# A two-layer graph network on one core: edge coefficients kept between two passes, shorter leftovers, and one edge tile in 75 fetched row by row from SyncE's queue

## The chip, the cores and the metric

The kernel runs on one core of a Trainium2 chip. The metric is device time in microseconds (us) of one execution. The engines are TensorE (PE; its weight loads are written PEld), VectorE (DVE), ScalarE (ACT), GpSimd (POOL) and SyncE (SP). "SPq" and "ACTq" in the profile are the instruction queues of SP and ACT, from which plain DMAs are issued; DMAs with an index list are issued by POOL.

## The reference

There are 30,000 nodes with 128 features and 960,000 edges, sorted by destination. Layer 0 has two relation passes, layer 1 one gate pass; each has a sum over edges by destination.

```
def _rel_graph_conv(h, basis, coeff, bias, src, dst, etype, norm):
    W = einsum('rb,bdf->rdf', coeff, basis)        # 32 relations of 8 bases
    msg = einsum('nd,rdf->nrf', h, W)[src, etype] * norm
    return segment_sum(msg, dst) + bias

h = max(layernorm(x), 0)
x = x + rel(relu(rel(h, basis1, coeff1, bias1)), basis2, coeff2, bias2)
h = max(layernorm(x), 0)
for t in range(4):
    eta = sigmoid((h @ Wk[t] + bk[t])[dst] + (h @ Wq[t] + bq[t])[src])
    agg = segment_sum(where(type4 == t, eta * (h @ Wv[t] + bv[t])[src], 0), dst)
    outs.append(agg + h @ Ws[t] + b[t])
x = x + mean(outs)
```

Both relation passes use the same sources, destinations, 32 edge types and edge weights; only the table of node rows, the bases and the 32 x 8 coefficients differ.

## The kernel before

**Tiles and groups.** An edge tile is 128 edges, a group is G = 3 tiles, a block is S = 5 groups, a stage is 5 blocks (25 groups, 75 tiles), and a turn of the loop is 4 stages (100 groups). A pass is a loop of 25 turns (L312). There are three passes, each made by `edge_pass` (L296): "c1" and "c2" with `rel_body` (L367), and "g" with `gate_body`. Turns go from the highest destinations to the lowest. The sums stay in SBUF, in the tile `agg`, with features on partitions and nodes along the free dimension.

**A group of a relation pass** (L438 to L467). POOL gathers three tiles of 128 rows into `hg` (L442, through the helper at L114); there are five `hg` buffers. DVE builds for each tile `sb`, a one-hot of the destination within a 32-node window times the 8 basis coefficients of each edge (L446). PE multiplies `hg` with `sb` into `pa` (L452), ACT copies `pa` into `ab` (L456). Once a block, PE multiplies the 8 bases into `po` (L414), and DVE adds the five windows into `agg` (L365).

**The coefficients of a block** (L383 to L409). SP loads the edge types, repeated over 32 partitions, into `er` (two buffers, L385); DVE compares them with the partition's number (L392); PE multiplies this one-hot with the coefficient table into `cp` (L397); DVE multiplies with the edge weights into `ce` (L406). The load is issued two blocks ahead. Both passes do this.

**Beside the edges.** Each turn also finishes ten blocks of 120 nodes whose sums are complete, one step at a time between the groups (`beside`, L323): after c1, ReLU and the row store to `h1`; after c2, layer norm and the matmuls that make the tables `ktab` and `qvtab`, which ACT's queue stores (L660); after g, the store of the output (L698). What is left after the last turn, 1440 nodes or 12 blocks, is done behind the loop, block by block (L328 to L332), before the next pass begins.

**What orders the work.** Each engine runs its instructions in the order in which this code names them. At the start of a stage SP loads the indices (`idx`), window positions (`relc`), weights (`nrm`) and window bases (`firsts`) of the next stage; the first stage's are loaded at the start of the turn (L419). At the third block of a stage each engine waits until all engines have left the stage before (L433). Waits are set by the recording layer. Each DMA that SP or ACT issues is given one of eight completion counters (called DMAHW0 to DMAHW7 in the built program) in turn, over both queues, and waits until the last DMA of that counter is complete; the counters are a set for each stage.

Of the kernel before, what the change touches and what calls it, by code (L numbers as in the profile page):

```python
# [9 lines left out]
F32 = mybir.dt.float32  # L10
I32 = mybir.dt.int32
# [7 lines left out]
P = 128  # L19
D = 128  # L20
# [27 lines left out]
LAG = 2 * VB  # L48
NX = N + NPI + LAG
GAP = 8  # L50
EPS = 1e-5
CH = 5
IN_RANGE = "destinations are node numbers, below N"
# [16 lines left out]
def kernel(  # L70
# [40 lines left out]
    qidx = nc.dram_tensor("qidx", (TP, NT), I32, kind="Internal").ap()  # L111

# [30 lines left out]
    basis, coeff = [], []  # L143
    for i, (bas, cof) in enumerate(((basis1, coeff1), (basis2, coeff2))):
        ct = consts.tile([P, 4, B], F32, name=f"coeff{i}")
        nc.vector.memset(ct, 0.0)
        for q in range(4):
            nc.scalar.dma_start(ct[q * R:(q + 1) * R, q, :], cof)
        basis.append(bas)
        coeff.append(ct)  # L150
# [34 lines left out]
    with tc.tile_pool(name="prep", bufs=2) as prep, tc.tile_pool(name="pre", bufs=4) as pre, \  # L185
# [52 lines left out]
        last = prep.tile([NI, 1], F32, name="last", bufs=1)  # L238
        nc.vector.tensor_reduce(last, at, AX.X, ALU.max)
        even = prep.tile([NI, 1], F32, name="even", bufs=1)  # L240
        nc.gpsimd.iota(even, pattern=[[0, 1]], base=N + LAG - W, channel_multiplier=-NPI,
                       allow_small_or_imprecise_dtypes=True)
        late = prep.tile([NI, 1], F32, name="late", bufs=1)
        nc.vector.tensor_tensor(late, last, even, ALU.is_gt)
# [4 lines left out]
    n_bad = nc.values_load(flag[0:1, 0:1], min_val=0, max_val=2 * CH * TP + NI)  # L249
# [44 lines left out]
    def sorted_path():  # L294
        with ExitStack() as all_:
            def edge_pass(name, body, after, banks, extra=None):  # L296


                with ExitStack() as held:
                    weights = held.enter_context(tc.tile_pool(name=f"{name}_w", bufs=1))  # L300
                    steps, run = after(weights), body(weights)
                    with tc.tile_pool(name=f"{name}_io", bufs=NQ) as io, \
                            tc.tile_pool(name=f"{name}", bufs=2) as pool, \
                            tc.tile_pool(name=f"{name}_n", bufs=1) as npool, \
                            tc.tile_pool(name=f"{name}_nps", bufs=banks, space=PSUM) as nps, \
                            tc.tile_pool(name=f"{name}_c", bufs=1, space=PSUM) as cps, \
                            tc.tile_pool(name=f"{name}_ps", bufs=2, space=PSUM) as ps:
                        cp = cps.tile([P, 4 * D], F32, name="cp")
                        iw, ic = cp[:, :W], cp[:, W:W + 1]
                        nc.vector.tensor_copy(iw, irow)  # L310
                        nc.vector.tensor_copy(ic, icol)
                        with tc.For_i(0, NI, 1, iteration_sync="staggered") as i:  # L312
                            with tc.manual_schedule():
                                todo = {}
                                for n, step_ in extra(i, npool) if extra else ():
                                    todo.setdefault(n, []).append(step_)
                                for u in range(NPI // VB):
                                    at = i * -NPI + (N + LAG + u * VB)
                                    for n, step in steps(at, npool, nps):
                                        todo.setdefault(u * PERIOD + n, []).append(step)  # L320
                                assert W < TQ * 4 * B and max(todo) < NG
# [6 lines left out]
                    with tc.tile_pool(name=f"{name}_l", bufs=3) as lpool, \  # L328
                            tc.tile_pool(name=f"{name}_lps", bufs=6, space=PSUM) as lps:
# [26 lines left out]

            def edge_row(row, i, s, n):
# [9 lines left out]
            def rel_body(table, weights, cof):  # L367
# [5 lines left out]
                def body(bas, i, io, pool, ps, cp, iw, ic, beside):  # L373
                    stage = {}
                    er, oh, pc, ce, ab, po, base = {}, {}, {}, {}, {}, {}, {}

                    def loads(k):
                        stage[k] = [stage_tile(io, "idx", src, I32, i, k),
                                    stage_tile(io, "relc", reld, F32, i, k),
                                    stage_tile(io, "nrm", norm, F32, i, k, 4 * TQ - S * G),  # L380
                                    firsts(io, i, k)]

# [7 lines left out]
                    def onehot(s):  # L390
                        oh[s] = pool.tile([P, TQ, TP], F32, name="oh")
                        nc.vector.tensor_scalar(oh[s], er[s], icol4, None, op0=ALU.is_equal)  # L392
                        at = (1 + s % 2) * TQ * 4 * B
                        pc[s] = cp[:TP, at:at + TQ * 4 * B].rearrange("p (c q b) -> p c q b",
                                                                      c=TQ, q=4)
                        for c in range(TQ):
                            nc.tensor.matmul(pc[s][:, c].rearrange("p q b -> p (q b)"),  # L397
                                             lhsT=oh[s][:, c, :],
                                             rhs=cof.rearrange("p q b -> p (q b)"),
                                             start=True, stop=True)  # L400

                    def coefficients(s):
                        ce[s] = pool.tile([TP, 4, TQ, B], F32, name="ce")
                        t0 = s % SB * S * G
                        nrm = stage[s // SB][2][:, t0:t0 + 4 * TQ]
                        nc.vector.tensor_mul(  # L406
                            ce[s], pc[s].rearrange("p c q b -> p q c b"),
                            nrm.rearrange("p (q c) -> p q c", q=4).unsqueeze(3).to_broadcast(
                                [TP, 4, TQ, B]))  # L409
# [10 lines left out]
                    types(0)  # L420
                    onehot(0)
                    coefficients(0)
                    types(1)
                    onehot(1)
                    for s in range(NS):
# [8 lines left out]
                        idx, relc, _, start = stage[k]  # L434
                        if s + 2 < NS:
                            types(s + 2)
                        ab[s] = pool.tile([P, B, S, W], F32, name="ab")
                        for g in range(S):  # L438
                            t0 = (s % SB * S + g) * G
                            hg = pool.tile([TP, G, D], F32, name="hg", bufs=5)  # L440
                            for j in range(G):
                                gather(hg[:, j, :], table, idx[:, t0 + j:t0 + j + 1])  # L442
                            pa = ps.tile([P, B, W], F32, name="pa", bufs=3)
                            for j in range(G):
# [4 lines left out]
                                    ce[s].rearrange("p q c b -> p (q c) b")[  # L449
                                        :, g * G + j, :].unsqueeze(2).to_broadcast([TP, B, W]),  # L450
                                    op0=ALU.is_equal, op1=ALU.mult)
                                nc.tensor.matmul(pa.rearrange("p b w -> p (b w)"),  # L452
                                                 lhsT=hg[:, j, :],
# [5 lines left out]
                            if g == 2 and s + 1 < NS:  # L459
                                coefficients(s + 1)  # L460
                            if g == 3 and s + 2 < NS:
                                onehot(s + 2)
# [100 lines left out]
            def after_first(weights):  # L563

                def steps(at, pool, ps):
                    xt = pool.tile([VB, D], F32, name="xt", bufs=2)
# [27 lines left out]
            def after_second(weights):  # L594
# [9 lines left out]
                def steps(at, pool, ps):  # L604
                    cols, rows = agg[:, ds(at, VB)], ds(at, VB)
                    xs = pool.tile([P, VB], F32, name="xs", bufs=2)
# [73 lines left out]
            def after_third(weights):  # L680

                def steps(at, pool, ps):
# [51 lines left out]
            edge_pass("c1", rel_body(h0, basis[0], coeff[0]), after_first, 2, codes)  # L734
            edge_pass("c2", rel_body(h1, basis[1], coeff[1]), after_second, 2)
# [3 lines left out]
    def any_path():  # L739
        with ExitStack() as all_:  # L740
# [60 lines left out]
            def rel_conv(table, to, weights, cof, relu):  # L801
                bas = cs.tile([P, B, D], F32, name="bas", bufs=2)
                nc.scalar.dma_start(bas, weights.rearrange("b d f -> d b f"))
                with tc.tile_pool(name="slow", bufs=2) as pool, \
# [18 lines left out]
                    for j in range(G):  # L823
                        nc.tensor.matmul(pc[:, j, :], lhsT=oh[:, j, :], rhs=cof[:R, 0], start=True,
                                         stop=True)
# [24 lines left out]
            rel_conv(h0, agg1, basis[0], coeff[0], False)  # L850
            rel_conv(agg1, agg2, basis[1], coeff[1], True)
# [117 lines left out]
```

## Time and profile before

| what | value |
|---|---|
| median of 3 runs | 28697.99 us (28687.42 to 28701.98) |
| the profiled execution: time | 28695.83 us |
| the profiled execution: span | 28694.1 us |
| first gather of c1, of c2, of g | 193.03, 9671.56, 19211.24 us |
| last gather of c1, of c2, of g ends | 9627.03, 19087.42, 28665.14 us |
| mean granted TensorE clock | 0.725 |
| DMA queues: of POOL's gathers; of SP; of ACT | 26.3%, 10.8%, 3.1% of 16 engines |

The span is the time from the first to the last instruction in the profile; the execution's time has 1.7 us more. In a group's line of the profile, "busy, mean ns" is the time in which the engine worked on it, and "idle before" is the time in which the engine stood just before it, with what ended most of that. "issue" means that the profile shows nothing that the engine waited for. A timeline line has the start in us, the duration, the engine and the line, and in brackets the idle time before it.

### The profile page before, as it was taken

The numbers are of one execution on the slowest core, as the hardware profiler recorded it, in microseconds if no ns is written. First come the engines' busy times: TensorE is split into PE (matmuls) and PEld (weight loads), VectorE is DVE, ScalarE is ACT, GpSimd is POOL, SyncE is SP. The second block draws the span as 40 slices with busy tenths as digits, with TensorE's granted clock in tenths as the row PEclk, the third lists the DMA queues.
The fourth block names the chain that finished last, engine by engine and source line by source line (L and its number), as shares of the span: only waits on it lengthen the run. The fifth ranks groups of instructions, "written<-read, shape, count | busy, mean of one in ns | idle before, by whom it ended". The sixth has DMA issues, their size and how long they took to land. (4 is left out here: it accounts for less than half of the span.)

```text
span 28694.1 us, 321544 instructions
## 1 busy us (share of the span) xinstructions
PE 21423.9 (75%) x87408; PEld 17175.0 (60%) x87408; DVE 12662.0 (44%) x33274; ACT 3718.3 (13%) x9905; POOL 21329.2 (74%) x22514
## 2 busy tenths in 40 slices
PE   5777777777777777777777777777777777777777
PEld 3555555555555555555555555556666666666666
DVE  4444444444444444444444444444444444444444
ACT  2111111111111111111111111111111111111111
POOL 5777777777777777777777777767777777777777
PEclk8888888888888888888888888875555555555555
DMA  4222222222222333333333333335555555555555
GB/s 113 73 74 73 73 75 74 74 74 74 74 73 74 80 88 88 88 88 88 88 87 88 87 87 88 87 107 177 176 177 177 177 176 176 177 177 177 177 177 168
DMA packets 2183600, 3244.39 MB, mean 113 GB/s; under 512 B 552518, under 2 KB 1560194, under 8 KB 2181890
## 3 DMA queue, kind: packets, MB, share of 16 engines
q0 software_dynamic: 840000, 1967.52, 26.3%
q1 hardware_dynamic: 994220, 1001.69, 10.8%
q10 hardware_dynamic: 347670, 254.20, 3.1%
q8 instruction: 852, 13.96, 0.2%
q14 instruction: 858, 7.03, 0.1%
HBM read 2969.33 MB, written 252.28 MB: 112 GB/s over the span
## 5 line engine op out<-in xcount | busy, mean ns | idle before, releaser
L114 POOL DMA_INDIRECT hg<-h,idx x15000 | 14212.2, 947 | 4846.7 <-issue 3865.1
L452 PE MATMUL pa<-sb,hg 128*128 128x256 f32 x30000 | 9879.9, 460 | 4210.1 <-DMA hg<-h,idx 2911.0
L452 PEld LDWEIGHTS pa<-sb,hg 128*128 128x128 f32 x30000 | 6016.4, 223 | 7340.5 <-issue 3683.7
L114 POOL DMA_INDIRECT qv<-qvtab,qi x7500 | 7089.3, 945 | 2488.5 <-issue 2063.6
L446 DVE SCALAR_TENSOR_TENSOR sb<-cp,relc,ce 128x256 f32<-128x256 f32 x15000 | 6145.4, 476 | 5311.9 <-PE cp L397 4980.1
L517 PE MATMUL po<-sel,msg 128*128 128x32 f32 x15000 | 3551.9, 393 | 2400.1 <-DVE msg L515 2394.2
L517 PEld LDWEIGHTS po<-sel,msg 128*128 128x128 f32 x15000 | 3396.6, 326 | 2839.2 <-DVE msg L515 2794.1
L506 PE MATMUL pk<-kw,kb 128*128 128x128 f32 x15000 | 3976.0, 438 | 137.1 <-DVE kb L493 137.1
L456 ACT COPY ab<-pa 128x256 f32<-128x256 f32 x5000 | 1860.4, 372 | 16420.0 <-PE pa L452 16227.4
L547 DVE TENSOR_TENSOR pk<-pk,qv 128x384 f32<-128x384 f32 x2500 | 1414.5, 566 | 5017.8 <-DMA qv<-qvtab,qi 3929.8
L506 PEld LDWEIGHTS pk<-kw,kb 128*128 128x128 f32 x15000 | 3468.2, 331 | 139.9 <-issue 139.9
L414 PEld LDWEIGHTS po<-ab,bas 128*128 128x128 f32 x16000 | 2859.8, 230 | 144.7 <-ACT ab L456 50.8
L414 PE MATMUL po<-ab,bas 128*128 128x160 f32 x16000 | 2883.9, 344 | 23.1 <-ACT ab L456 23.1
L365 DVE TENSOR_TENSOR agg<-agg,po 128x32 f32 x7500 | 1403.2, 187 | 1972.8 <-PE po L414 861.4
L548 ACT ACTIVATE pk<-pk 128x384 f32<-128x384 f32 x2500 | 1187.3, 476 | 7774.6 <-DVE pk L547 7739.7
L397 PEld LDWEIGHTS cp<-coeff,oh 128*128 128x128 f32 x8000 | 1313.8, 235 | 452.5 <-issue 328.0
L397 PE MATMUL cp<-coeff,oh 128*128 128x32 f32 x8000 | 1229.3, 304 | 358.8 <-DVE oh L392 358.8
L515 DVE TENSOR_TENSOR msg<-pk,qv 128x384 f32<-128x384 f32 x2500 | 1368.1, 548 | 0.0
L493 DVE TENSOR_TENSOR kb<-kb,cp 128x1920 f32<-128x1920 f32 x500 | 1072.6, 2145 | 46.7 <-issue 29.5
L644 PE MATMUL bank<-wall,hT 128*120 128x512 f32 x1572 | 911.2, 697 | 9.0 <-issue 4.6
L655 DVE TENSOR_TENSOR kt<-bank,ball 120x512 f32<-120x512 f32 x262 | 181.1, 691 | 924.7 <-PE bank L644 924.7
L392 DVE TENSOR_SCALAR oh<-er,icol 128x512 f32<-128x512 int32 x1000 | 490.6, 491 | 88.8 <-issue 62.7
(77 smaller groups left out, 3548.1 us busy)
## 6 DMA issues: line engine op xcount, KB each, us to landing
kb<-kcode SPq DMA_DIRECT2D x500, 960.0 KB
er<-in_et_row SPq DMA_DIRECT2D x1000, 256.0 KB
hg<-h,idx POOLq DMA_INDIRECT x15000
kw<-ktab SPq DMA_DIRECT2D x2500, 64.0 KB
qvtab<-qvt ACTq DMA_DIRECT2D x262, 480.0 KB, 4.3
qv<-qvtab,qi POOLq DMA_INDIRECT x7500
ktab<-kt ACTq DMA_DIRECT2D x262, 240.0 KB, 3.3
xt<-in_x SPq DMA_DIRECT2D x262, 60.0 KB, 5.0
```

The lines of the kernel that those rows point to most:

```text
L114: nc.gpsimd.indirect_dma_start(out=to, out_offset=None, in_=table, in_offset=bass.IndirectOffsetOnAxis(ap=idx, axis=0))
L365: nc.vector.tensor_add(to, to, po[:, g, :])
L397: nc.tensor.matmul(pc[s][:, c].rearrange("p q b -> p (q b)"), lhsT=oh[s][:, c, :], rhs=cof.rearrange("p q b -> p (q b)"), start=True, stop ...
L414: nc.tensor.matmul(po[s].rearrange("p s w -> p (s w)"), lhsT=bas[:, b, :], rhs=ab[s][:, b].rearrange("p s w -> p (s w)"), start=(b == 0), ...
L446: nc.vector.scalar_tensor_tensor(sb, iw[:TP].unsqueeze(1).to_broadcast([TP, B, W]), relc[:, t0 + j:t0 + j + 1], ce[s].rearrange("p q c b - ...
L452: nc.tensor.matmul(pa.rearrange("p b w -> p (b w)"), lhsT=hg[:, j, :], rhs=sb.rearrange("p b w -> p (b w)"), start=(j == 0), stop=(j == G ...
L456: nc.scalar.copy(ab[s][:, :, g, :], pa)
L506: nc.tensor.matmul(pk[n][:, j, :], lhsT=kb[n // S][:, n % S, j * TP:(j + 1) * TP], rhs=kw[n], start=True, stop=True)
L515: nc.vector.tensor_mul(msg, pk[n], qv[n][:, :, 1, :])
L517: nc.tensor.matmul(po[s][:, g, :], lhsT=msg[:, j, :], rhs=sel[s][:, g * G + j, :], start=(j == 0), stop=(j == G - 1))
L547: nc.vector.tensor_add(pk[n], pk[n], qv[n][:, :, 0, :])
L548: nc.scalar.activation(pk[n], pk[n], AF.Sigmoid)
```

## The change

1. **Coefficients of both passes in c1.** The coefficient table gets both layers' columns, so the matmul of L397 is 64 columns wide instead of 32. DVE multiplies twice, into `ce0` for c1 and `ce1`, which ACT's queue stores to a new DRAM tensor `ce2` once a block. c2 loads its coefficients from there (`kept`, on SP's queue, four buffers) and has no types, one-hots or coefficient matmuls.
2. **Edges reversed group by group** and not turn by turn, with node blocks following closer behind. 480 nodes (4 blocks) are left after each loop instead of 1440 (12 blocks), and their steps are interleaved over the four blocks, with up to 8 PSUM buffers. The check on first destinations, which chooses between the sorted path and a general one, is made for every group.
3. **One tile in 75 by rows.** The last tile of each stage in c1 and c2 isn't gathered by POOL. SP loads its 128 indices into one partition, loads them 16 at a time into registers, and issues 128 DMAs of one row (512 bytes) each, in eight parts of 16 at groups 1, 3, 6, 8, 11, 13, 16 and 18 of the stage. The tile goes to `hx` (two buffers), which the last matmul of the stage's last group reads.

The core of the diff:

```diff
-LAG = 2 * VB
-NX = N + NPI + LAG
+LAG = 4 * VB
+NX = N + LAG
+XR = 16
...
+            def row_loader(io, pool, table, array, i, k):
+                ix = io.tile([1, TP], I32, name="ix")
+                nc.sync.dma_start(
+                    ix, array[:, ds(i * (NQ * NTS) + (k + 1) * NTS - 1, 1)].rearrange("p o -> o p"))
+                got = pool.tile([TP, D], F32, name="hx")
+
+                def fetch(c):
+                    _, vals = nc.values_load_multi_w_load_instructions(
+                        ix[:, c * XR:(c + 1) * XR], engines=[SP], min_val=0,
+                        max_val=table.shape[0] - 1,
+                        skip_runtime_bounds_check_because=IN_RANGE)
+                    for p, v in enumerate(vals):
+                        nc.sync.dma_start(got[c * XR + p:c * XR + p + 1, :], table[ds(v, 1), :])
...
+                    def one_by_one(k, n):
+                        if n == 0:
+                            rest[k] = row_loader(io, pool, table, src, i, k)
+                        for c in range(TP // XR):
+                            if n == (c * (NGS - 5)) // (TP // XR) + 1:
+                                rest[k][1](c)
...
+                        for to, l in ((ce, 0), (ce_next, 1)):
+                            to[s] = pool.tile([TP, 4, TQ, B], F32, name=f"ce{l}")
+                            nc.vector.tensor_mul(
+                                to[s], pc[s][:, :, :, l].rearrange("p c q b -> p q c b"),
...
+                    def keep(s):
+                        nc.scalar.dma_start(block_rows(s), ce_next[s][:, :S * G, :].rearrange(
+                            "p t b -> p (t b)"))
+
+                    def kept(s):
+                        ce[s] = pool.tile([TP, S * G, B], F32, name="ce", bufs=4)
+                        nc.sync.dma_start(ce[s].rearrange("p t b -> p (t b)"), block_rows(s))
...
                             hg = pool.tile([TP, G, D], F32, name="hg", bufs=5)
+                            rows = [hg[:, j, :] for j in range(G)]
+                            if t0 + G == NTS:
+                                rows[-1] = rest[k][0]
                             for j in range(G):
-                                gather(hg[:, j, :], table, idx[:, t0 + j:t0 + j + 1])
+                                if t0 + j + 1 < NTS:
+                                    gather(rows[j], table, idx[:, t0 + j:t0 + j + 1])
...
-                        for at in range(0, NPI + LAG, VB):
-                            for _, step in steps(at, lpool, lps):
+                        for together in zip(*(steps(at, lpool, lps, left)
+                                              for at in range(0, LAG, VB))):
+                            for _, step in together:
                                 step()
```

More of the change, by code (lines that the diff above doesn't have):

```diff
@@ L47 @@
 PERIOD = NG * VB // NPI - 1
-LAG = 2 * VB
-NX = N + NPI + LAG
+LAG = 4 * VB
+NX = N + LAG
+LEAD = 3 * VB
 GAP = 8
 EPS = 1e-5
+XR = 16
 CH = 5
-IN_RANGE = "destinations are node numbers, below N"
+IN_RANGE = "the edges' ends are node numbers, below N"
 def rows_of(col, n):
@@ L111 @@
     qidx = nc.dram_tensor("qidx", (TP, NT), I32, kind="Internal").ap()
+    ce2 = nc.dram_tensor("ce2", (NI * NS, TP, S * G * B), F32, kind="Internal").ap()
     def gather(to, table, idx):
@@ L141 @@
     nc.vector.memset(eps, EPS)
[L143 to L146, printed above, removed]
+    basis = basis1, basis2
+    coeff = consts.tile([P, 4, 2, B], F32, name="coeff")
+    nc.vector.memset(coeff, 0.0)
+    for i, cof in enumerate((coeff1, coeff2)):
         for q in range(4):
-            nc.scalar.dma_start(ct[q * R:(q + 1) * R, q, :], cof)
-        basis.append(bas)
-        coeff.append(ct)
+            nc.scalar.dma_start(coeff[q * R:(q + 1) * R, q, i, :], cof)
     def normalised(pool, xt, kn, name, p=P):
@@ L237 @@
         nc.sync.dma_start(at, first.rearrange("(i g) -> i g", i=NI))
[L238 to L242, printed above, removed]
+        even = prep.tile([NI, NG], F32, name="even", bufs=1)
+        nc.gpsimd.iota(even, pattern=[[-NPI // NG, NG]], base=N + LAG - LEAD - W,
+                       channel_multiplier=-NPI, allow_small_or_imprecise_dtypes=True)
+        nc.vector.tensor_tensor(even, at, even, ALU.is_gt)
         late = prep.tile([NI, 1], F32, name="late", bufs=1)
-        nc.vector.tensor_tensor(late, last, even, ALU.is_gt)
+        nc.vector.tensor_reduce(late, even, AX.X, ALU.add)
         nc.vector.tensor_add(nbad[:NI], nbad[:NI], late)
@@ L294, in sorted_path @@
     def sorted_path():
+        for u in range(NPI // VB):
+            late = min(g for g in range(NG)
+                       if min((g // S + 2) * S + S - 2, NG) > u * PERIOD + 1)
+            assert (u + 1) * VB - late * NPI // NG <= LEAD
         with ExitStack() as all_:
@@ L317, in edge_pass @@
                                 for u in range(NPI // VB):
-                                    at = i * -NPI + (N + LAG + u * VB)
-                                    for n, step in steps(at, npool, nps):
+                                    at = i * -NPI + (N + LAG - (u + 1) * VB)
+                                    for n, step in steps(at, npool, nps, 2):
                                         todo.setdefault(u * PERIOD + n, []).append(step)
-                                assert W < TQ * 4 * B and max(todo) < NG
+                                assert W < TQ * 8 * B and max(todo) < NG
                                 def beside(n):
@@ L365, in add_windows, with rel_body @@
                     nc.vector.tensor_add(to, to, po[:, g, :])
-            def rel_body(table, weights, cof):
+            def rel_body(table, weights, second):
                 def start(npool):
@@ L374, in body @@
                     stage = {}
-                    er, oh, pc, ce, ab, po, base = {}, {}, {}, {}, {}, {}, {}
+                    er, oh, pc, ce, ce_next, ab, po, base, rest = {}, {}, {}, {}, {}, {}, {}, {}, {}
                     def loads(k):
@@ L379, in loads @@
                                     stage_tile(io, "relc", reld, F32, i, k),
-                                    stage_tile(io, "nrm", norm, F32, i, k, 4 * TQ - S * G),
                                     firsts(io, i, k)]
+                        if not second:
+                            stage[k].append(
+                                stage_tile(io, "nrm", norm, F32, i, k, 4 * TQ - S * G))
+                    def one_by_one(k, n):
[4 more added lines that the diff above has]
+                                rest[k][1](c)
                     def types(s):
@@ L402, in coefficients @@
                     def coefficients(s):
-                        ce[s] = pool.tile([TP, 4, TQ, B], F32, name="ce")
                         t0 = s % SB * S * G
[L405 to L409, printed above, removed]
+                        nrm = stage[s // SB][-1][:, t0:t0 + 4 * TQ]
@@ L419, in body @@
                     loads(0)
[L420 to L424, printed above, removed]
+                    if second:
+                        kept(0)
+                        kept(1)
+                    else:
+                        types(0)
+                        onehot(0)
+                        coefficients(0)
+                        types(1)
+                        onehot(1)
                     for s in range(NS):
@@ L433, in body @@
                             leave_stage()
-                        idx, relc, _, start = stage[k]
+                        idx, relc, start = stage[k][:3]
                         if s + 2 < NS:
-                            types(s + 2)
+                            (kept if second else types)(s + 2)
                         ab[s] = pool.tile([P, B, S, W], F32, name="ab")
@@ L458, in body @@
                                 bases_out(s - 1)
-                            if g == 2 and s + 1 < NS:
+                            if g == 2 and not second and s + 1 < NS:
                                 coefficients(s + 1)
-                            if g == 3 and s + 2 < NS:
-                                onehot(s + 2)
+                            if g == 3 and not second:
+                                keep(s)
+                                if s + 2 < NS:
+                                    onehot(s + 2)
                             if g == 3 and s > 1:
@@ L680, in after_third, with steps @@
             def after_third(weights):
-                def steps(at, pool, ps):
+                def steps(at, pool, ps, deep):
                     c = pool.tile([P, VB], F32, name="c")
@@ L823, in rel_conv @@
                     for j in range(G):
-                        nc.tensor.matmul(pc[:, j, :], lhsT=oh[:, j, :], rhs=cof[:R, 0], start=True,
+                        nc.tensor.matmul(pc[:, j, :], lhsT=oh[:, j, :], rhs=cof, start=True,
                                          stop=True)
@@ L917, in edges @@
     def edges(v):
-        return np.ascontiguousarray(v.reshape(NI, -1)[::-1]).reshape(-1)
+        return np.ascontiguousarray(v.reshape(NGR, GE)[::-1]).reshape(-1)
     def by_tile(v):
```

45 lines of the change are left out of this document (26 added, 19 removed).

## The prediction, made before the changed kernel ran

> **What bounds the kernel.** First the page's busy table and its costliest groups. No engine is near full, yet GpSimd (POOL) has a row of its own kind:
>
> ```profile
> PE 21423.9 (75%) x87408; PEld 17175.0 (60%) x87408; DVE 12662.0 (44%) x33274; ACT 3718.3 (13%) x9905; POOL 21329.2 (74%) x22514
> ...
> L114 POOL DMA_INDIRECT hg<-h,idx x15000 | 14212.2, 947 | 4846.7 <-issue 3865.1
> ...
> L114 POOL DMA_INDIRECT qv<-qvtab,qi x7500 | 7089.3, 945 | 2488.5 <-issue 2063.6
> ```
>
> 22,500 gathers of 947 ns busy and about 0.30 us between them. POOL's timeline in mid pass shows that the 0.30 is no wait but the pace itself:
>
> ```profile
> 5000.97 0.94 POOL L114 DMA_INDIRECT hg<-h,idx  x1 [0.30 <-issue]
> 5002.22 0.94 POOL L114 DMA_INDIRECT hg<-h,idx  x1 [0.31 <-issue]
> 5003.47 0.95 POOL L114 DMA_INDIRECT hg<-h,idx  x1 [0.30 <-issue]
> ```
>
> First to last gather, the first relation pass (c1) takes 9434.0 us (193.03 to 9627.03), the second (c2) 9415.9 (9671.56 to 19087.42), the gate pass 9453.9: 1.256 us a gather, 3.77 a group of three. These three stretches and the gaps of 44.5 and 123.8 us between them are the span. So POOL's gathers bound all three passes, and what counts is any time that POOL must wait.
>
> **What goes.** (a) One gather in 75 in c1 and c2: 200 x 1.256 = **-251 us**, all of it on the path. (b) The node blocks left after each loop go from 12 to 4 and are interleaved. In the gap before the gate pass 12 blocks run one behind the other from 19097.8 to 19198.4, 100.6 us. Four together keep the first block's 3.4 us up to its first L644, four times about 4.8 us of PE work (six L644 rows of 697 ns and the small ones) and an end of some 5 us: about 28, so -72. The gap before c2 has 16.8 us of blocks (9636.1 to 9652.9), the end 14.4 (28675.8 to 28690.2); a third of each plus one chain leaves 6 and 5: -11 and -9. Together **-92 us**.
>
> **What is hidden.** c1 gets a second multiplication per block (L406 takes 0.28 us), wider coefficient matmuls (L397, 304 ns each) and a store; c2 loses L392, L397, L406 and 500 loads of 256 KB. All are on engines that idle in every block (DVE 44% busy), so nothing either way; if c1's DVE cover were gone, 500 x 0.28 = 140 us. As traffic, 25,600 rows of 512 B and c2's 500 coefficient loads come, 128 MB of type loads go; POOL's waits for landed gathers are 265 us in 702 times, 53 us beyond the 0.30 pace, so about 50 us could come or go, and I take nothing.
>
> **What is added: SP's rows.** Each stage of 25 groups gets 128 one-row loads and 8 register loads on SP. The nearest rows are SP's other one-row load, its register loads and its loads with a computed address:
>
> ```profile
> L348 SPq DMA_DIRECT2D firsts<-in_first_st x300: 249/253/1192, 191.1 to 28463.0; - x150
> L348 SPq FUSED_REGOPS  x275: 51/60/60, 190.9 to 28462.9; - x138
> ```
> ```profile
> L352 SPq TENSOR_LOAD <-firsts x100: 1821/1838/2022, 19211.1 to 28551.6; - x100
> ```
> ```profile
> 24030.24 2.46 SPq L490 DMA_DIRECT2D kw<-ktab  x5
> ...
> 24090.69 0.29 SPq L348 DMA_DIRECT2D firsts<-in_first_st  x1
> 24091.19 0.35 SPq L342 DMA_DIRECT2D qi<-qidx  x1
> ```
>
> The one-row load is issued in 0.25 us; with its register steps and gaps the next follows 0.46 to 0.50 later (0.50 above; the 0.33-us loads after it come 0.54 apart). I take **0.47 us a row**. Bounds: its own pieces without gaps, 0.25 + 0.06 + 0.03 = 0.34; the kw loads, five in 2.46 us, 0.53. A register load of 25 values takes 1.84, one of a single value 0.47, so 16 values 1.33 (estimate). A stage costs SP 128 x 0.47 + 8 x 1.33 + about 10 for its other loads and the landing of ix = 81 us of POOL's 74 x 1.256 = 92.9. Taken alone it fits.
>
> **The wait that comes with them.** The list of the built program shows what the diff doesn't. Each DMA of SP or ACT gets one of eight completion counters in turn, over both queues, and waits for its counter's last DMA. The turns were dealt as if the rows were slower than 0.47: in c2's first stage ACT's stores of group 18 (ktab) and 19 (qvtab) stand between rows 53 and 57, though the program fetches those rows at group 8. Row 64 waits for counter 6 at 144, and the qvtab store raises it from 128 to 144. So row 64 can't go before ACT has finished group 19, and 64 rows are behind it in SP's queue. PE waits for the last row at group 24; POOL, with five hg buffers, at group 30 (24 + 6).
>
> Store times: ACT copies a group 3.3 us after its last gather starts (9626.09, matmul 9628.69, copy 9629.40 for 0.37), so a store after group n is issued at 3.77(n+1) + 2.4 from the stage's first gather, and lands 4.3 later (qvtab's median), 2.6 for the small one (as qidx).
>
> ```profile
> qvtab<-qvt ACTq DMA_DIRECT2D x262, 480.0 KB, 4.3
> ...
> ktab<-kt ACTq DMA_DIRECT2D x262, 240.0 KB, 3.3
> ```
>
> Then the rows left, their register loads and coefficient loads (0.55 each), 2.2 to land (estimate; the quiet one-row load at 19208.18 had moved its packets by 19209.5, xt takes 5.0), and 2.4 for PE to free the buffer (copies follow each other by 1.4 us when PE catches up near 600). POOL wants that buffer at 89 x 1.256 = 111.8.
> - c2 stage 0, row 64 behind group 19: 77.8 + 4.3 + 65 rows 30.6 + 5.3 + 1.1 + 2.2 + 2.4 = 123.7; late by **11.9**.
> - stage 1, row 83 behind group 21: 85.4 + 4.3 + 46 rows 21.6 + 2.7 + 0.5 + 4.6 = 119.1; **7.3**.
> - stage 2, row 88 behind group 23: 92.9 + 4.3 + 41 rows 19.3 + 2.7 + 0.5 + 4.6 = 124.3; **12.5**.
> - stage 3, row 67 behind group 16: 66.5 + 4.3 + 62 rows 29.1 + 4.0 = 103.9. Only now does SP loop back (1.9, as PE's branch at L312 takes 1.86; SP's, now short, 0.06) and load the next turn's idx, 2.6 to land: 108.5. POOL wants it at 92.9; **15.6**.
> - c1 has small stores, and its stages 0 to 2 come out before 111.8 (the nearest, stage 0, by 5). In stage 3 row 101 waits for group 23: 92.9 + 2.6 + 28 rows 13.2 + 1.3 + 1.9 + 2.6 = 114.5; **21.6**. In the run of before SP has the next idx issued at 519.93, 50 us ahead of POOL; this cover is what goes.
>
> Twenty-five turns: c1 25 x 21.6 = **+540**, c2 25 x 47.3 = **+1183**.
>
> **Sum:** 28694 - 251 - 92 + 540 + 1183 = 30074, and 1.7 outside the span (the profiled execution took 28695.83; the median of before is 2.2 higher): **30,080 us**, +4.8%. 242 rows a turn lie behind a hold, so each 0.01 us of row spacing is 60 us: 0.34 gives 29,290, 0.53 gives 30,440; stores landing 1 us later add some 125. The likeliest case's own range is 29,300 to 30,600.
>
> Against this stands a rule. The trace's one-row load is issued in 253 ns. The Trainium skill's page "DMA: Bandwidth & Descriptors", in its section on the anatomy of one DMA, puts the sequencer's dispatch at about 50 ns and the rest of the fixed 2 us into completion. At 50 ns a row the holds of c2 would vanish and only some 10 us a turn of c1 be left, and the sum would be about 28,600; but that table is of the GpSimd path, and the row decides.
>
> **Rivals.** (1) *Faster: the holds end before POOL needs anything.* Place: SP's rows behind the held one. It decides at a spacing of about 0.2 us: c2's four waits are gone below 0.29, 0.31, 0.17 and 0.22. c1's loop wait stays at 8 us even with free rows (+210), so this gives about 28,600. For it: 0.25 is the issue itself, and gaps could overlap. Against: every SP row shows the gap. 6%; another 3% for 0.2 to 0.34, near 28,900. (2) *SP itself becomes the bound*: if a row lands as late as xt does (5.0 us), eight counters allow one per 0.63, c1's stage needs some 100 us, and the time is 31,050 to 31,600. Against: a row is one packet and its completion, xt 120 rows of 512 B behind a 256-KB load. 10%. (3) *The sorted path isn't taken*, the new check on first destinations being per group: many times slower. The bound leaves 88 nodes of room at the first group, where destinations end at 29,999. 1%.
>
> **How the numbers follow.** Likeliest 80%. Range 29,300 to 30,900: the likeliest case and the start of rival 2. 0.2% is about what can be told from no change here: faster 7%, within 0.2% 2%, slower 91%.
>
> **What would show it.** POOL should have about 25 waits of some 22 us in c1, each on idx at a turn's start, and about 100 of 7 to 16 us in c2, on PE and idx; 14,800 hg gathers at still 1.25; SP's rows 0.47 apart, with one long wait per stage on a store of ACT. The gap before the gate pass should shrink to some 65 us (-72, +13 for the last rows). Wrong if POOL shows no such waits, or SP's rows follow at 0.3.

## The result and the profile after

The changed kernel takes **30,243.2 us** (median of 4 runs, 30,232.4 to 30,261.3) against 28,695.8 before: ratio 1.0541, interval 1.0524 to 1.0557. The profiled execution took 30,261.25, its span is 30,259.5. Forecast were 30,080 and 29,300 to 30,900.

Runs are compared only with runs of the kernel before on the same chip, because the chips differed here: on some the kernel before takes 28,660 to 28,700 us, as in the result, on others 34,150 to 34,210. Each experiment says which it met. The experiments met five chips, each in one session, so no run shows whether such a difference stays with a chip.

The busy row and POOL's two groups of the page after:

```profile
PE 20156.3 (67%) x83304; PEld 16554.4 (55%) x83304; DVE 12434.8 (41%) x32709; ACT 3707.2 (12%) x9841; POOL 21110.7 (70%) x22314
...
L117 POOL DMA_INDIRECT hg<-h,idx x14800 | 13993.2, 945 | 6717.1 <-issue 3709.3
...
L117 POOL DMA_INDIRECT qv<-qvtab,qi x7500 | 7090.6, 945 | 2411.0 <-issue 2045.6
```

A gather is about as long as before (945 ns, before 947) and there are 200 fewer, but POOL's idle time ahead of hg went from 4846.7 to 6717.1 us. POOL's waits, in all, times and longest, say who ends it:

```profile
POOL hg L117 <- PE pa L508: 1370.5, 1223, 12.0
POOL hg L117 <- PE po L462: 680.4, 710, 20.7
POOL hg L117 <- DMA idx<-in_src: 366.4, 25, 48.1
...
POOL hg L117 <- PE bank L695: 163.2, 39, 7.1
...
POOL qv L117 <- DMA qi<-qidx: 48.5, 1, 48.5
```

Most of the 1223 and 710 are the 0.30 us between gathers, listed under the engine that happened to finish last; what counts is in the longest. From POOL's timeline, one turn of c1 (4311.4 to 4718.7) has waits of 19.3 us at its start and of 6.1, 1.5, 4.1, 3.3 and 2.3 in between; one of c2 (14,190.8 to 14,600.6) 13.5 at its start and 10.4, 6.3 and 11.3 later. The wait at the start of a c1 turn is listed as one for PE L462, but PE was long done: the next turn's idx was issued at 4715.44 and POOL went on at 4718.67.

What held SP back stands in SP's own waits:

```profile
SPq L378 <- DMA ktab<-kt: 1910.0, 201, 20.9
SPq L378 <- DMA ce<-ce: 1590.6, 384, 10.7
...
SPq L373 <- DMA ix<-in_src: 646.5, 198, 7.2
SPq L457 <- DMA ktab<-kt: 562.7, 25, 24.3
SPq L378 <- DMA h<-h: 436.3, 146, 6.4
SPq L378 <- DMA qvtab<-qvt: 362.7, 184, 4.1
```

L378 fetches rows of h0 or h1. It reads neither ktab, qvtab nor ce, and the h store that it waits for in c1 is h1's, while its rows are h0's; yet 4,300 us of its waiting (1,910.0 + 1,590.6 + 436.3 + 362.7) end with a store that ACT issued, and a coefficient load (L457) waits 562.7 for ktab as well. Such a wait is called a hold here. The trace has each DMA's completion counter as well: in all 915 of these holds of rows, the last DMA that was issued on the row's own counter is the store of ACT that the wait names. For instance, ACT issued a ktab store on counter 184 (the trace's number) at 14,267.04, and the row that SP issued at 14,270.37 was on 184 and waited for it. This is the shared completion counter at work.

### The profile page after: what moved, and what is told of

Same layout as the page of the kernel before. It is cut to its first block, busy times and chain, and to the rows that moved or that the text cites. A ratio compares the mean times of both kernels' runs of the same rounds, so it can differ in the third digit from the quotient of the medians.

```text
span 30259.5 us, 394591 instructions
## 1 busy us (share of the span) xinstructions
PE 20156.3 (67%) x83304; PEld 16554.4 (55%) x83304; DVE 12434.8 (41%) x32709; ACT 3707.2 (12%) x9841; POOL 21110.7 (70%) x22314
## 4 chain that ended last, share of the span: by engine, by line
## 5 line engine op out<-in xcount | busy, mean ns | idle before, releaser
L117 POOL DMA_INDIRECT hg<-h,idx x14800 | 13993.2, 945 | 6717.1 <-issue 3709.3
L508 PE MATMUL pa<-sb,hg 128*128 128x256 f32 x29600 | 9116.4, 451 | 2274.5 <-DMA hg<-h,idx 1000.8
L508 PEld LDWEIGHTS pa<-sb,hg 128*128 128x128 f32 x29600 | 6186.8, 225 | 4649.7 <-issue 2213.1
L462 PEld LDWEIGHTS po<-ab,bas 128*128 128x128 f32 x16000 | 2541.1, 208 | 128.8 <-ACT ab L512 59.2
L462 PE MATMUL po<-ab,bas 128*128 128x160 f32 x16000 | 2585.0, 319 | 23.1 <-ACT ab L512 23.1
L432 PE MATMUL cp<-coeff,oh 128*128 128x64 f32 x4000 | 836.7, 379 | 2537.5 <-DVE oh L427 2537.1
L432 PEld LDWEIGHTS cp<-coeff,oh 128*128 128x128 f32 x4000 | 773.9, 285 | 2699.6 <-DVE oh L427 2458.2
L427 DVE TENSOR_SCALAR oh<-er,icol 128x512 f32<-128x512 int32 x500 | 251.5, 503 | 3936.9 <-DMA er<-in_et_row 3936.5
L508 PE MATMUL pa<-sb,hx 128*128 128x256 f32 x400 | 221.1, 655 | 2088.4 <-DMA hx<-h 2088.4
L508 PEld LDWEIGHTS pa<-sb,hx 128*128 128x128 f32 x400 | 108.7, 310 | 2161.2 <-issue 2149.3
```

Of the source, the lines that this page charges most:

```text
L117: nc.gpsimd.indirect_dma_start(out=to, out_offset=None, in_=table, in_offset=bass.IndirectOffsetOnAxis(ap=idx, axis=0))
L432: nc.tensor.matmul(pc[s][:, c].rearrange("p q l b -> p (q l b)"), lhsT=oh[s][:, c, :], rhs=coeff.rearrange("p q l b -> p (q l b)"), start= ...
L462: nc.tensor.matmul(po[s].rearrange("p s w -> p (s w)"), lhsT=bas[:, b, :], rhs=ab[s][:, b].rearrange("p s w -> p (s w)"), start=(b == 0), ...
L508: nc.tensor.matmul(pa.rearrange("p b w -> p (b w)"), lhsT=rows[j], rhs=sb.rearrange("p b w -> p (b w)"), start=(j == 0), stop=(j == G - 1))
```

## What the experiments show

**Stores of ACT on SP's queue (four runs of one kernel).** Every store that ACT issued in the loops of c1 and c2 is issued by SP, so no row can wait for a store that is written after it.

```
-                        nc.scalar.dma_start(block_rows(s), ce_next[s]...
+                        nc.sync.dma_start(block_rows(s), ce_next[s]...
...
-                        nc.scalar.dma_start(h1[rows, :], h)
+                        nc.sync.dma_start(h1[rows, :], h)
...
-                            nc.scalar.dma_start(table[rows, :]..., t)
+                            nc.sync.dma_start(table[rows, :]..., t)
```

(kcode's and qidx's stores likewise.)

> All rows as in the changed kernel, but every store that ACT issued in the loops of both relation passes is issued by SP, so that one queue holds all their DMAs in the written order and no row can stand behind a store that is written after it. Theory (the holds): no waits at a turn's start, none on late rows; 28,696 - 251 - 77 = 28,370, up to 28,450 if SP's longer list shows. Rival 1 (SP is the bound by its 25,600 row issues): SP gets about 50 more issues a turn, so not below 30,240. Rival 2 (SP's loads of edge types, behind rows in the same queue, hold the first pass whatever the stores do): the first pass keeps its 15 us a turn in mid turn, about 28,750.

> ACT's stores of both relation passes issued by SP once more, wanted on a chip where the kernel before takes about 28,700 us; in the run on record before this one it took 34,147 there, and SP's rows followed each other by some 0.6 us instead of 0.41. Theory (the holds), at 0.41 us a row: no wait at a turn's start and none on late rows, 28,370 to 28,450. Rival 1 (SP bound by its issues even at 0.41): not below 30,240. On a chip where rows follow at 0.6 again: SP alone needs more than a stage of POOL, and the time stays about 13% above before, as the run on record gave.

> ACT's stores of both relation passes issued by SP, rows as in the changed kernel (addresses from registers), once more in want of a chip where the kernel before takes about 28,700 us and SP's rows follow at 0.41. Theory (holds): with fixed rows the same move took the last wait away (9.4 us a turn); here it should take all waits of 34.6 and 41.3 us a turn: 28,300 to 28,450, up to 28,700 if edge types and stores behind rows cost a few us a turn. Rival (SP bound by its instructions at 0.41 us a row, not by holds): not below 30,240. Where before takes 34,150: 38,600 again.

> ACT's stores of both relation passes issued by SP, rows as in the changed kernel; the last try to get it beside a kernel before of about 28,700 us. Theory (holds) there: 28,300 to 28,700. Rival (SP bound at 0.41 us a row): not below 30,240. Where before takes 34,150: 38,550.

The last run met a chip with 28,666.8 us before: **28,234.9 us**, ratio 0.9849 (0.9833 to 0.9866). This is the fastest kernel of the study. It has all 25,600 rows, and 32 more issues of SP in a turn of c1 and 20 in one of c2. SP's and POOL's waits there:

```profile
SPq L373 <- DMA ix<-in_src: 485.4, 172, 6.6
SPq L718 <- DVE sb L503: 415.0, 134, 8.6
```
```profile
POOL hg L117 <- issue: 3659.9, 11461, 165.7
...
POOL hg L117 <- PE pa L508: 203.8, 634, 2.3
```

The rows' waits for stores are gone; SP now waits at a store (L718) whose data isn't ready, in the order in which it was written. No wait of POOL inside c1 or c2 is over 2.3 us. So the loss was not SP's work: in the changed kernel SP waits 104 us of a c1 turn of 409 and 119 of a c2 turn of 410, which leaves 305 and 291 us of its own, less than POOL's 371. Rival 2 falls on chips of this kind; what it started from, rows that wait till earlier rows have landed, is 24.4 us in the whole changed kernel.

On three other chips, where before takes 34,147, 34,207 and 34,187, the same kernel took 38,564, 38,633 and 38,542 (ratios 1.1294, 1.1289 and 1.1274): there moving the stores helps little. Where both ran on one chip, it is 38,633 against 38,844 for the changed kernel (one run). Why is seen next.

**The changed kernel on such a chip.**

> The changed kernel itself, on the chip of these runs. Where the kernel before takes about 28,700: 30,240. Where it takes about 34,150: rows at some 0.6 us need 4 x 100 us and more of SP in a turn of 372, so about 37,500 to 38,500 whatever the holds do.

38,844 against 34,207 (one run, no interval). SP's waits there:

```profile
SPq L378 <- DMA ce<-ce: 372.4, 145, 11.2
...
SPq L378 <- DMA ktab<-kt: 102.0, 14, 9.0
```

and SP's rows in its timeline, 32 rows in c1, first on this chip, then on that of the result, both without a hold of note:

```profile
6007.35 23.40 SPq L378 DMA_DIRECT2D hx<-h  x32
```
```profile
4399.75 14.63 SPq L378 DMA_DIRECT2D hx<-h  x32
```

The same 32 rows and the register load between them take 23.4 us instead of 14.6. SP's single DMA keeps its 225 ns, but 11,115 times a next instruction of SP starts 0.65 to 0.75 us after the end of the one before, against 50 times on the other chip. The stores have mostly landed before SP comes to a row, and the holds shrink to 595 us. SP waits only 38 us of a c1 turn of 547 and 15 of a c2 turn of 535, so on this chip SP is the bound. That is what rival 2 said, but not for its reason: rows wait 256 us in all for the landing of earlier rows, and what is long are the gaps between instructions. POOL stalls too on such a chip, here in the kernel with all tiles gathered (described below):

```profile
POOL hg L117 <- remote: 2133.6, 850, 4.8
```

"Remote" is a wait that no engine or DMA of the core ends; 571 of the 850 are 2.5 us or more, often 22 us apart. The granted TensorE clock is lower over the whole of the changed kernel on this chip (0.654 against 0.699), but that isn't what makes the time: in the gate pass, where it is 0.51 on both, the pass takes 11,500 us against 9,453. No run shows why instructions come late on these chips.

**Rows from fixed addresses, with the stores on ACT and on SP.** Rows 0 to 127 of the table are fetched, so the part of the computation that is changed is whose rows the last tile of a stage gets; ix, its register loads and the register steps of a row go.

```
-                    _, vals = nc.values_load_multi_w_load_instructions(...)
-                    for p, v in enumerate(vals):
-                        nc.sync.dma_start(got[c * XR + p:c * XR + p + 1, :], table[ds(v, 1), :])
+                    for p in range(c * XR, (c + 1) * XR):
+                        nc.sync.dma_start(got[p:p + 1, :], table[p:p + 1, :])
```

> The changed kernel, but the 128 rows of a tile are read from fixed addresses (rows 0 to 127 of the table, so the last tile of a stage gets other nodes' rows: the addresses that depend on the edges are left out, with ix, its register loads and the register steps of each row). A row is then one instruction of SP. Order and stores of ACT stay, so the holds stay. Theory (holds): rows at 0.25 to 0.28 us shorten what follows a hold by 41 to 65 rows x 0.14 = 6 to 9 us, and of 34.6 and 41.3 us a turn some 20 and 11 stay: 28,370 + 25 x 31 = 29,150 where before takes 28,700. Where before takes 34,150 (SP's other instructions come late there and the rows cost SP about 0.6 us each): SP is no longer the bound, and between 33,700 and 34,700, by how much of the holds is left. Rival (SP bound by instructions, no holds): the same time as the next kernel, within 100 us.

> The same fixed rows (the same part of the computation changed), and ACT's stores of both relation passes issued by SP: no holds and few instructions. Both theories: before less 251 and less 77, scaled where before takes longer: 28,370 where it takes 28,700, and 33,700 where it takes 34,150. The theory of the holds expects the kernel with the stores on ACT to be slower than this one by 400 to 900 us; the rival expects both alike.

Both met a chip with 28,661.8 before: 28,473.4 (0.9933, 0.9917 to 0.9950) and 28,255.8 (0.9857, 0.9841 to 0.9874). The stores on SP save 217.6 us with fixed rows, half of the 400 that I had set as the least, and the first kernel is some 680 us faster than I expected. The timeline of the first shows 16 rows without a hold, and POOL's one long wait of a turn, at a c1 turn's start:

```profile
4316.06 4.69 SPq L371 DMA_DIRECT2D hx<-h  x16
```
```profile
4378.89 0.94 POOL L117 DMA_INDIRECT hg<-h,idx  x1 [9.37 <-PE po L455]
```

A row each (4.69 - 0.22) / 15 = 0.30 us. A pass has 24 such starts, on average of 9.78 us: 24 x (9.78 - 0.30) = 228, about the 217.6 that the second kernel saves. The holds are still there, and longer (its rows wait 2,650 us for ce and 2,542 for ktab), but what follows a hold is now short enough to be done before POOL wants it, except in c1's last stage, whose last hold ends with the turn. So here a hold cost by the time of what stands behind it, not by its own length.

**All tiles gathered.** The rows are off; the other two parts of the change, kept coefficients and short loops, stay.

```
-                                if t0 + j + 1 < NTS:
-                                    gather(rows[j], table, idx[:, t0 + j:t0 + j + 1])
+                                gather(rows[j], table, idx[:, t0 + j:t0 + j + 1])
-                            one_by_one(k, s % SB * S + g)
```

> The union with all 75 tiles of a stage gathered by POOL: kept coefficients and short loops behind each pass stay, the rows on SP go. Theory (SP's rows, held behind ACT's stores, are the whole loss): 28,696 of before less what the gaps between the passes gave in the changed kernel, 3.6 - 75.3 - 9.1 + 4.0 = -77, so 28,620, and passes of 9,420 to 9,435 us as before. Rival (the second multiplication, the wider coefficient matmuls and the kept store cost something themselves in the first pass): above 28,690, with the first pass longer than its 9,434.0.

33,932 against 34,147: 0.9931 (0.9915 to 0.9948), on a chip with late instructions. These two parts cost nothing there. The gain of 215 us is more than the 77 expected, and this chip doesn't tell what it would be on the other: the second pass also loses its one-hots and coefficient matmuls, and fewer instructions may count more where they come late (argued, not shown).

**Rows without the last stage, and one stage ahead.** In the first, stage 3 is gathered. In the second, stage k fetches the tile that stage k+1 uses in its ninth group; stage 0's is gathered.

```
+                            if k < NQ - 1:
+                                one_by_one(k, s % SB * S + g)
...
+                            if k + 1 < NQ:
+                                one_by_one(k + 1, s % SB * S + g)
```

> The changed kernel without rows in the last stage of a turn (its last tile is gathered): SP reaches the next turn's idx load unheld. Theory: the waits at a turn's start go (19.3 us in the first pass, 13.3 in the second, 25 turns each: -815), 50 gathers come back (+63): 29,490; mid-turn waits stay. Rival (the loss is SP's own work, even over stages): a quarter of the two passes' loss goes, (812 + 831 + 251) / 4 = 470, so 29,770.

> Rows are fetched one stage ahead (SP fetches in stage k the tile that stage k+1 uses in its ninth group), in stages 0 to 2 alone; stage 0's tile is gathered, so 150 of the 200 gathers go. ACT's stores stay where they are. Every held row then has about 30 us of time more than it is late. Theory, if late rows are all that counts: 28,696 - 150 x 1.256 - 77 = 28,430. Theory, if what stands behind the held rows in SP's queue counts too (edge types in the first pass, needed by the one-hot of a block two blocks on): the first pass keeps some 11 of its 15 us a turn in stages 0 to 2, so about 28,700. Rival (SP bound by issues): the three stages with rows lose what they lost, about 29,400.

Both met late instructions: 37,434 (1.0963, 1.0944 to 1.0981) and 36,941 (1.0814, 1.0796 to 1.0832), beside 1.1294 for the kernel with all rows and the stores on SP on the same chip. Both leave out a quarter of the rows, and the second also gives the others a stage's time more. Each takes part of the loss away; neither tells of the holds, and on the first kind of chip neither ran.

**Edge types one block earlier in c1 (two runs).** A third er buffer, loaded three blocks ahead.

```
-                        if s + 2 < NS:
-                            (kept if second else types)(s + 2)
+                        if second and s + 2 < NS:
+                            kept(s + 2)
+                        if not second and s + 3 < NS:
+                            types(s + 3)
```

> The changed kernel with the first pass's edge types loaded one block (five groups, 18.8 us) earlier into a third buffer; rows, stores and holds stay. Theory (in the first pass the waits of stages 0 to 2, 15 us a turn, come from edge types that stand in SP's queue behind held rows, 10 to 17 us late, and not from the rows): 25 x 15 = 380 us go, 29,860. Rival (they come from the late rows themselves): no change, 30,240. The waits at the turn's start stay in both, and so does the second pass.

> Edge types of the first pass one block earlier, rows, stores and holds as in the changed kernel, in want of the same chip. Theory (the first pass's waits of stages 0 to 2, 15 us a turn, come from edge types behind held rows): 25 x 15 us less, 29,860. Rival (they come from late rows): 30,240. Where before takes 34,150: 39,270 again.

Twice a chip with late instructions: 39,268 (1.1474, 1.1454 to 1.1493) and 39,200 (1.1468, 1.1448 to 1.1487). On the first of these chips that is 424 us above the changed kernel, though DVE's wait for edge types fell from 5,798.8 us there to 205.2:

```profile
DVE oh L427 <- DMA er<-in_et_row: 5798.8, 355, 31.3
```
```profile
DVE oh L427 <- DMA er<-in_et_row: 205.2, 48, 15.8
```

PE's wait for one-hots went with it, from 2,852.1 to 35.5 us, so there the late types were its cause; but its wait for xt, the rows of the node blocks, which SP loads too, rose from 1,208.7 to 3,798.7. Where SP is the bound, the lateness only moved from one of its loads to another. What the edit would give on the chip of the result, it doesn't say.

## Why the prediction came out near, and where it was wrong

First to last gather, c1 takes 10,245.9 us (197.0 to 10,442.9), c2 10,247.1 (10,491.0 to 20,738.1), the gate pass 9,453.0. Term by term, the 251 us of the gathers that went given back to each pass in equal parts:

| term of the sum | forecast | measured |
|---|---|---|
| 200 gathers | -251 | -251 (at 1.256) |
| waits in c1 | +540 | 811.9 + 125.6 = +937 |
| waits in c2 | +1183 | 831.2 + 125.6 = +957 |
| start, gaps, gate pass, end | -92 | +4.0 + 3.6 - 75.3 - 0.9 - 9.0 = -78 |
| sum | +1380 | +1565 |

- **The bound**: right. POOL's pace stayed at 945 + 300 ns, and what was lost is POOL's waits. With the waits gone (stores on SP, all rows) c1 and c2 take 9,275.0 and 9,238.1 us, 337 less than before: the 251, some 50 of shorter waits between gathers, which I had counted as possible and taken nothing for, and some 40 of gathers that are 944.8 ns on average instead of 947.4.
- **The mechanism**: right, and tested: the holds. In c2's first stage row 64, which I had waiting for a qvtab store till 82.1 us after the stage's first gather, went at 82.1 (14,272.89 - 14,190.77), on the counter of that store; row 60 had been held before it by a ktab store, till 79.6. Rows 83 and 88 in the next two stages and row 101 in c1's last are held as forecast, too; in c2's last stage it was row 64 and not 67. The waits of 11.9, 7.3, 12.5 and 15.6 were 10.4, 6.3, 11.3 and 13.5: each 1 to 2 us less. Main reason: a row takes 0.41 us, not 0.47. Two lines show it, 16 rows with no hold and the issue itself:

```profile
4471.78 6.40 SPq L378 DMA_DIRECT2D hx<-h  x16
```
```profile
L378 SPq DMA_DIRECT2D hx<-h x25600: 219/225/1549, 211.6 to 20747.5; - x199
```

(6.40 - 0.22) / 15 = 0.41; over 41 to 65 rows that is 2.5 to 3.9 us a hold. The register load of 16 is 1.23 (taken 1.33), and the landing of ix, which I had in the "about 10" of a stage, is waited for 19.3 us in a c1 turn and 5.7 in a c2 turn, four times each.
- **c1 at the turn's start**: 21.6 forecast, 19.3 measured (19.6 on average), for the same reason: 28 rows in 12.55 us, then the loop back, then 3.2 from issue of idx to POOL's next gather. A pass has 24 such waits, not 25, because nothing stands before its first turn.
- **The step that failed**: "its stages 0 to 2 come out before 111.8". I asked only when the *rows* of c1 land. The rows alone were judged rightly: in c1 PE waits for rows only in the last group of a turn, 25 times in all. But behind a held row stand other loads in SP's queue, and in c1 each block has one of edge types, for the block after the next, with a one-hot and the coefficient matmuls behind it. One case, by engine, the wait at 4408.71:

```profile
4374.01 23.14 SPq L378 DMA_DIRECT2D hx<-h  x32
4397.43 0.59 SPq L420 DMA_DIRECT2D er<-in_et_row  x1
```
```profile
4402.41 0.49 DVE L427 TENSOR_SCALAR oh<-er,icol 128x512 f32<-128x512 int32 x1 [16.50 <-DMA er<-in_et_row]
```
```profile
4402.95 1.97 PE L432 MATMUL cp<-coeff,oh 128*128 128x64 f32 x8 [11.14 <-DVE oh L427]
```
```profile
4408.71 0.94 POOL L117 DMA_INDIRECT hg<-h,idx  x1 [6.07 <-PE pa L508]
```

Rows that 32 x 0.41 and a register load would have put into 14.6 us took 23.1 through holds; the er load left only then; DVE's one-hot waited 16.5 us for it, PE's coefficient matmul, in PE's order ahead of the next groups, 11.1 for the one-hot, and POOL 6.1 for a buffer. PE had done 19 groups of the stage; its row tile is wanted in the 25th. In all PE's wait for one-hots rose from 358.8 us in both passes to 2537.1 in c1 alone, and that for xt, which stands in the same queue, from 7.9 to 474.0 in c1. The line before, and PE's waits after up to the end of c1:

```profile
L397 PE MATMUL cp<-coeff,oh 128*128 128x32 f32 x8000 | 1229.3, 304 | 358.8 <-DVE oh L392 358.8
```
```profile
PE cp L432 <- DVE oh L427: 2537.1, 377, 146.6
PE bank L640 <- DMA xt<-in_x: 474.0, 120, 6.6
PE pa L508 <- DMA hx<-h: 332.5, 25, 14.1
```

The five waits of stages 0 to 3 in this turn are 17.3 us, less the pace 15.8, and this turn has few: all 25 turns together have 516 us of waits beyond the pace within them, where the kernel before had 38 in c1. The 24 waits at a turn's start give 463. So c1's 937 is 463 in place of 540, and some 475 that I had put at nothing. For the chip of the result the traces show this chain, and that late rows have no part in it; the edit that should have tested the edge types alone met other chips. That the stores on SP leave 453.2 of the 2537.1 agrees with it.
- **Several holds a stage in c1**: I expected one long one. Its rows waited 15 times for ce and 5 for h in a turn, 63.3 and 16.5 us, up to 9.3. Small stores didn't make for small holds; by the order of the issues, what counts is when ACT issues them (no run tests this alone).
- **Luck**: c2's 226 too much and c1's 397 too little cancel in part, so that the total, 163 us too low, is closer than its larger parts.
- **Tails**: with late rows out of the way (stores on SP) the gap before c2 is 34.2 us, that before the gate pass 40.4: -10 and -83 against -11 and -72. In the changed kernel the last rows give 14 and 8 of it back (48.1 and 48.5, where I had expected 65 for the second); I had given 13 for the second alone.
- **Rival 1** put the decision at about 0.2 us a row and a remaining wait of 8 us a turn in c1 on free rows. With fixed rows at 0.30 c2's waits were all gone and c1's was 9.4. So its place was right; whether its point lies higher than 0.2 isn't shown, because with fixed rows the register loads, 2.7 to 5.3 us of a hold in the sum, and ix are gone as well. At 0.41 it fails.
- **The rule of the Trainium skill** (page "DMA: Bandwidth & Descriptors", the anatomy of one DMA): a sequencer's dispatch of about 50 ns, for DMAs that GpSimd issues. On SP's queue the row's DMA is issued in 225 ns, and rows follow at 0.41, or 0.30 without register steps. No run here shows 50 ns for SP; the measurement decides.

## What to carry to other kernels

A DMA that shares its completion counter with a store of another engine waits for that store, though it has no data in common with it; with many small DMAs on one queue, list for each counter who raised it last, and price a hold by everything that stands behind it in the queue, not only by the transfers that you added. Where such holds decide, put the stores on the same queue in the order in which they become ready: here that turned +5.4% into -1.5% with the same work. And before a queue is loaded with many instructions, find out how fast instructions come on the chips it will run on.

## What was not expected of the hardware

- The chips differed by 19% on the kernel before (28,660 to 28,700 against 34,150 to 34,210 us). The profiles of both kinds have equal gathers (945 to 948 ns), equal issues of rows (225 ns) and, in the changed kernel, equal busy time of PE (20,163 and 20,156 us): the difference lies between instructions. It changes which rival holds, from the holds to SP's own pace, and a change that gains 1.5% on one loses 13% on the other (rows with the stores on SP).
- A one-row DMA with a fixed address follows the last at 0.30 us, with an address from a register at 0.41: the two register steps (37 and 29 ns) and their gaps are the difference, though the DMA itself is issued in 225 ns then and in 250 with a fixed address.
- A load of 128 single words of 4 bytes (ix) makes SP wait up to 7.2 us, 4.8 on average in a c1 turn (19.3 in 4), behind 256-KB loads of edge types in the same queue, and 1.4 in a c2 turn (5.7 in 4), behind coefficient loads of 60 KB. That the loads ahead of it make the difference is argued, not shown.
